# Mamba block of a four-layer graph network: rows of B and C by broadcast DMA instead of one-hot matmuls, dt products in four row groups of TensorE, and a scan that writes over its input

## The chip, the cores and the metric

The kernel runs on one core of a Trainium2 chip. The metric is the device time of the whole program in microseconds (us). The kernel before takes 3858.1 us, the median of three runs (3853.97 to 3861.62). The profile and the trace are of one execution whose span was 3854.7 us. PE is TensorE, PEld its weight loads, DVE is VectorE, ACT ScalarE, POOL GpSimd, and SP the engine whose queue issues the DMAs.

## The reference, cut to what matters

Four layers run one after the other on a graph of 3327 nodes with 256 features: a residual mean aggregation, a Mamba block behind a graph convolution, an attention layer, and two rounds of top-p attention. The change touches only the second. Its core, for a sequence of 3327 steps `t`, 512 channels `d` and 16 states `s`:

```python
h = layernorm(relu(adj @ x @ gcn_w + gcn_b))
xz = h @ w_in                       # 512 channels xc and 512 of a gate z
u = silu(causal_conv4(xc))
dbc = u @ w_xp                      # 16 columns for dt, 16 of B, 16 of C
dt = softplus(dbc[:, :16] @ w_dt + b_dt)
B, C = dbc[:, 16:32], dbc[:, 32:]
dA = exp(dt[:, :, None] * A[None])
dBu = dt[:, :, None] * B[:, None, :] * u[:, :, None]
# hst = dA_t * hst + dBu_t;  y_t = sum over s of hst[:, s] * C_t[s]
y = (ys + u * D_skip) * silu(z)
out = y @ w_out
```

All inputs are float32; in this block only the rows of B and C (see below) are kept in a shorter type.

## The kernel before

Channels lie on the 128 partitions, in four groups `g` of 128; time lies along the free axis. The 3328 (padded) steps are cut into eight chunks `c` of 128, 256, 384 and five times 512 steps (`ends`, lines 239 to 244). In each chunk the 16 states follow one another, so there are 128 pairs (chunk, state). For each pair:

- `row` (439 to 449) makes row `s` of B visible on all partitions. B and C are held as `parts`: three bfloat16 terms of each float32 number, 96 rows. One bfloat16 matmul with a one-hot stationary operand (a column of `three`) adds the three terms and copies the row to all 128 partitions in PSUM (445), and ACT copies it to SBUF (448). Rows are asked for two states ahead.
- `decay` (451 to 460) has POOL put the carried state into column 0 of each group of `db`, and ACT compute `dA = exp(A*dt)` in four activations.
- `feed` (462 to 466) is the DVE product `db = du * B` over 128 x 4w numbers, w being the chunk's width.
- `scan` (468 to 477) is one DVE recurrence over all four groups, which reads `dA` and `db` and writes `h`; POOL then copies the last column to `carry`. `dA`, `db` and `h` have two buffers each.
- `reader` (479 to 486) makes row `s` of C in PSUM by a matmul as above, and DVE multiplies `h` by it in place (549).
- Four pairs of half-matmuls against the identity add `h` to the chunk's sum in four PSUM banks `ys` (557).

Two kinds of work are woven in. `pump()` (322) advances the generator `convolve` by a step: it issues about nine of the 26 matmuls `adj @ x` of a tile of 128 nodes (264), whose operand `at` is loaded by SP (263, two buffers), then the product with `gcn_w`, the layer norm (POOL computes the power) and the transposition into `hT`. Once per state it is called, and at state 3 as often as the next chunk needs. `head(c + 1)` is advanced by one step at the end of states 3 to 14: input projection and convolution by group (four steps), then u and the 112-row product with `w_xp` (386), the split of B and C into the three terms (389 to 398 and 407: ACT casts, DVE subtractions), the dt product with `w_dt` (402, K = 16, one matmul for each group), and softplus on ACT and DVE. `gate` and `back` finish the chunk before.

PSUM has eight banks: four for `ys`, two for `ps` (rows of B, projections, `w_xp`, `w_dt`, transpositions, output product), one for `cb` of `convolve`, one for C. The framework orders instructions on each engine by the program and a priority; `tc.high_priority()` moves one ahead, `tc.keep_in_program_order` pins one. Each engine, and SP's DMA queue, runs its instructions in that order, and an instruction that waits holds those behind it. The order of the main loop is:

```python
if k < len(states): rows.append(row(*states[k]))     # k = two states ahead
if nxt: decay(*nxt)
h = scan(x, s)
...
if nxt: feed(*nxt, rows.pop(0))
nc.vector.tensor_mul(h, h, C.to_broadcast([P, NG, w]))
if nxt: C = reader(*nxt)
... # ys += h, back, gate_input, pump, head
```

Of the kernel before, what the change touches and what calls it, by code (L numbers as in the profile page):

```python
# [9 lines left out]
F32 = mybir.dt.float32  # L10
# [33 lines left out]
def gnn_kernel(ctx: ExitStack, tc: tile.TileContext, n: int, a: dict, out: bass.AP):  # L44
# [109 lines left out]
    with tc.tile_pool(name="l1b", bufs=1) as wpool, tc.tile_pool(name="l1at", bufs=2) as l1at:  # L154
# [33 lines left out]
        with tc.tile_pool(name="l1aw", bufs=1) as cwork, tc.tile_pool(name="l1c", bufs=2) as ch, \  # L188
                tc.tile_pool(name="l1t", bufs=3) as tmp, tc.tile_pool(name="l1s", bufs=2) as work, \
                tc.tile_pool(name="l1y", bufs=1, space=PSUM) as ypsum, \  # L190
                tc.tile_pool(name="l1p", bufs=2, space=PSUM) as psum, \
                tc.tile_pool(name="l1q", bufs=1, space=PSUM) as cpsum:
            def scratch():
                return tmp.tile([P, NG, 3 + WC], F32, name="t")

            gw = load(wpool, "gcn_w")
            w_dt = wpool.tile([6 * DS + DTR, DI], F32, name="w_dt")
            gb, one = w_dt[0:1, :D], w_dt[0:1, D:D + P]
# [16 lines left out]
            last = wpool.tile([P, NG, 3], F32, name="last")  # L215
            nc.vector.memset(last, 0.0)

            BC = 2 * DS
            w_sp = wpool.tile([P, NG, 3 * BC + DTR], F32, name="w_sp")
            nc.sync.dma_start(w_dt[3 * BC:, :], a["w_dt"])  # L220
            three = wpool.tile([3 * BC, BC], BF16, name="three")
            for k in range(3):
                nc.sync.dma_start(w_sp[:, :, k * BC:(k + 1) * BC], a["w_xp"][:, :, DTR:])
                nc.vector.tensor_copy(three[k * BC:(k + 1) * BC, :], ident[k * BC:(k + 1) * BC, k * BC:(k + 1) * BC])
            nc.sync.dma_start(w_sp[:, :, 3 * BC:], a["w_xp"][:, :, :DTR])

            wg = wpool.tile([P, 2, D + 2], F32, name="wg")
            nc.sync.dma_start(wg[:, :, :D], a["gat_w"])
# [16 lines left out]
            hTs, us, szs, splits = {}, {}, {}, {}  # L245

            def power(rs, var):

# [110 lines left out]
            def head(c):  # L359

                w = ends[c] - starts[c]
                xc = scratch()
                nc.gpsimd.tensor_copy(xc[:, :, :3], last)
                u = us[c] = ch.tile([P, NG, WC], F32, name="u", bufs=1)[:, :, :w]
                for g in range(NG + 1):
                    if g < NG:  # L370
                        nc.scalar.copy(xc[:, g, 3:3 + w], project(c, g, w))
# [12 lines left out]
                ps = psum.tile([P, WC], F32, name="ps")  # L384
                for g in range(NG):
                    nc.tensor.matmul(ps[:3 * BC + DTR, :w], w_sp[:, g, :], u[:, g, :],
                                     start=(g == 0), stop=(g == NG - 1))
# [12 lines left out]
                for g in range(NG):  # L400
                    ps = psum.tile([P, WC], F32, name="ps")
                    nc.tensor.matmul(ps[:, :w], w_dt[3 * BC:, g * P:(g + 1) * P], left[3 * BC:],
                                     start=True, stop=True)
                    nc.scalar.activation(v[:, g, :], ps[:, :w], AF.Identity, bias=b_dt[:, g:g + 1])
# [26 lines left out]

            dAs, dbs = ([cwork.tile([P, NG * (1 + WC)], F32, name=f"{x}{i}") for i in range(2)] for x in ("dA", "db"))

            def by_group(t, w):
                return t[:, :NG * (1 + w)].rearrange("p (g w) -> p g w", g=NG)

            def row(c, s):

                parts = splits[c]
                w = parts.shape[1]
                pb = psum.tile([P, WC], F32, name="ps")[:, :w]
                with tc.high_priority():
                    nc.tensor.matmul(pb, three[:, s:s + 1].to_broadcast([3 * BC, P]), parts, start=True, stop=True)
                B = work.tile([P, 1, WC], F32, name="row", bufs=2)[:, :, :w]
                with tc.high_priority():
                    nc.scalar.copy(B[:, 0, :], pb)  # L448
                return B

            def decay(x, s):

                c, dt, du = x
                w = dt.shape[2]
                dA, db = (by_group(x[s % 2], w) for x in (dAs, dbs))
                if s < 2 and (c == 0 or w != ends[c - 1] - starts[c - 1]):
                    nc.gpsimd.memset(dA[:, :, 0:1], 0.0)
                nc.gpsimd.tensor_copy(db[:, :, 0], carry[:, s, :])
                for g in range(NG):
                    nc.scalar.activation(dA[:, g, 1:], dt[:, g, :], AF.Exp, scale=A[:, g, s:s + 1])  # L460

            def feed(x, s, B):

                du = x[2]
                w = du.shape[2]
                nc.vector.tensor_mul(by_group(dbs[s % 2], w)[:, :, 1:], du, B.to_broadcast([P, NG, w]))  # L466

            def scan(x, s):

                w = x[2].shape[2]  # L470
                h = work.tile([P, NG * (1 + WC)], F32, name="h")
                m = NG * (1 + w)
                nc.vector.tensor_tensor_scan(h[:, :m], dAs[s % 2][:, :m], dbs[s % 2][:, :m],  # L473
                                             initial=0.0, op0=ALU.mult, op1=ALU.add)
                h = by_group(h, w)
                nc.gpsimd.tensor_copy(carry[:, s, :], h[:, :, w])
                return h[:, :, 1:]

            def reader(x, s):

                parts = splits[x[0]]
                w = parts.shape[1]
                C = cpsum.tile([P, 1, WC], F32, name="C")[:, :, :w]
                nc.tensor.matmul(C[:, 0, :], three[:, DS + s:DS + s + 1].to_broadcast([3 * BC, P]), parts,  # L484
                                 start=True, stop=True)
                return C

            def gate(c, ys):
                sz = szs[c]
# [39 lines left out]
            feed(x, 0, rows.pop(0))  # L529
            C = reader(x, 0)  # L530
            ys = ahead = None
            for c in range(nch):
                w = us[c].shape[2]
                for s in range(DS):
# [14 lines left out]
                    nc.vector.tensor_mul(h, h, C.to_broadcast([P, NG, w]))  # L549
# [781 lines left out]
```

## Time and profile before

| part of the span | from, to (us) | what |
|---|---|---|
| layer 0 | 0 to 366 | aggregation; bound by 26 x 26 matmuls of line 116 |
| layer 1 | 366 to 1641 | the stage of the change; scans (line 473) from 406.2 to 1611 |
| layers 2 and 3 | 1641 to 3855 | attention and top-p; untouched by the change |

| over the whole span | busy us | share |
|---|---|---|
| PE | 3499.9 | 91% |
| DVE | 2610.2 | 68% |
| ACT | 1738.5 | 45% |
| POOL | 494.7 | 13% |

A window's row gives, for each engine, busy time and number of instructions in that stretch, then the granted TensorE clock as a share of full speed, and DMA's share and rate. A row of the waits gives the waiting instruction, what it waited for, the total, the number of waits and the longest. A row of the timeline gives start, duration, engine, line, operation, and in brackets how long the engine had been idle and for whom. A float32 matmul stands in the trace as two records.

### The profile page before, as it was taken

The numbers are of one execution on the slowest core, as the hardware profiler recorded it, in microseconds if no ns is written. First come the engines' busy times: TensorE is split into PE (matmuls) and PEld (weight loads), VectorE is DVE, ScalarE is ACT, GpSimd is POOL, SyncE is SP. The second block draws the span as 40 slices with busy tenths as digits, with TensorE's granted clock in tenths as the row PEclk, the third lists the DMA queues.
The fourth block names the chain that finished last, engine by engine and source line by source line (L and its number), as shares of the span: only waits on it lengthen the run. The fifth ranks groups of instructions, "written<-read, shape, count | busy, mean of one in ns | idle before, by whom it ended". The sixth has DMA issues, their size and how long they took to land. (4 is left out here: it accounts for less than half of the span.)

```text
span 3854.7 us, 41751 instructions
## 1 busy us (share of the span) xinstructions
PE 3499.9 (91%) x15079; PEld 2593.0 (67%) x15079; DVE 2610.2 (68%) x5588; ACT 1738.5 (45%) x2612; POOL 494.7 (13%) x734
## 2 busy tenths in 40 slices
PE   8999999898889778689989999999999999999975
PEld 7888876554554434378868787777777667667664
DVE  1111579898988999877753445444454888888987
ACT  0000665554545465211122333333346777777773
POOL 0000122222221221111110000000001111111110
PEclk9999999998999888889999999999999999999997
DMA  7443211111111000044423222122203112221100
GB/s 231 139 134 95 84 59 53 37 46 36 42 36 36 6 0 0 15 158 139 148 73 88 62 61 56 51 59 62 59 11 101 58 56 63 64 63 54 58 23 7
DMA packets 100529, 252.96 MB, mean 66 GB/s; under 512 B 14786, under 2 KB 49090, under 8 KB 100178
## 3 DMA queue, kind: packets, MB, share of 16 engines
q1 hardware_dynamic: 100306, 250.13, 21.2%
q8 instruction: 122, 2.00, 0.2%
q14 instruction: 101, 0.83, 0.1%
HBM read 239.86 MB, written 10.22 MB: 65 GB/s over the span
## 5 line engine op out<-in xcount | busy, mean ns | idle before, releaser
L473 DVE TENSOR_TENSOR_SCAN h<-dA,db 128x2052 f32<-128x2052 f32 (+3 forms) x128 | 464.0, 3625 | 5.9 <-PE y L557 3.4
L460 ACT ACTIVATE dA<-dt,A_log 128x512 f32<-128x512 f32 (+3 forms) x512 | 297.0, 637 | 326.7 <-DVE h L473 272.7
L557 PE MATMUL y<-h,ident 128*128 128x512 f32 (+3 forms) x1024 | 436.1, 563 | 3.2 <-DVE h L549 3.2
L841 PE MATMUL acc<-G,wt 128*128 128x256 f32 x1352 | 332.7, 396 | 63.4 <-ACT wt L839 62.2
L557 PEld LDWEIGHTS y<-h,ident 128*128 128x128 f32 x1024 | 199.4, 207 | 258.0 <-issue 232.4
L839 ACT COPY wt<-tp 128x512 f32<-128x512 f32 (+1 forms) x364 | 185.9, 554 | 382.7 <-PE tp L837 382.4
L841 PE MATMUL acc<-X,wt 128*128 128x256 f32 x1352 | 343.8, 391 | 10.3 <-ACT wt L839 9.8
L841 PEld LDWEIGHTS acc<-G,wt 128*128 128x128 f32 x1352 | 254.1, 194 | 133.7 <-ACT wt L839 81.6
L809 PE MATMUL acc<-F,at 128*128 128x256 f32 x1352 | 323.1, 389 | 0.6 <-ACT q L604 0.6
L116 PE MATMUL acc<-xa,at 128*128 128x257 f32 x1352 | 310.1, 383 | 5.4 <-DMA at<-in_adjT 5.4
L841 PEld LDWEIGHTS acc<-X,wt 128*128 128x128 f32 x1352 | 242.3, 189 | 105.5 <-issue 41.3
L732 PE MATMUL acc<-F,at 128*128 128x257 f32 x1352 | 307.9, 384 | 4.9 <-DVE at L729 4.9
L264 PE MATMUL cb<-F,at 128*128 128x256 f32 x1352 | 310.6, 382 | 1.6 <-ACT hn L283 1.6
L809 PE MATMUL acc<-X,at 128*128 128x256 f32 x1352 | 309.4, 383 | 2.9 <-issue 2.9
L809 PEld LDWEIGHTS acc<-F,at 128*128 128x128 f32 x1352 | 253.8, 193 | 74.0 <-issue 40.0
L264 PEld LDWEIGHTS cb<-F,at 128*128 128x128 f32 x1352 | 257.3, 191 | 58.7 <-issue 17.7
L466 DVE TENSOR_TENSOR db<-du,row 128x2048 f32<-128x2048 f32 (+3 forms) x128 | 240.2, 1879 | 82.6 <-ACT row L448 82.5
L853 DVE MAX8 cand<-e 128x8 f32<-128x128 f32 x676 | 142.2, 281 | 226.4 <-ACT e L795 214.9
L116 PEld LDWEIGHTS acc<-xa,at 128*128 128x128 f32 x1352 | 256.7, 192 | 42.6 <-issue 5.4
L809 PEld LDWEIGHTS acc<-X,at 128*128 128x128 f32 x1352 | 255.0, 192 | 44.0 <-issue 10.9
L732 PEld LDWEIGHTS acc<-F,at 128*128 128x128 f32 x1352 | 256.4, 193 | 41.8 <-issue 5.1
L549 DVE TENSOR_TENSOR h<-h,C 128x2048 f32<-128x2048 f32 (+3 forms) x128 | 240.9, 1882 | 37.2 <-PE C L484 23.7
(305 smaller groups left out, 5303.6 us busy)
## 6 DMA issues: line engine op xcount, KB each, us to landing
at<-in_adjT SPq DMA_DIRECT2D x102, 832.0 KB, 4.5
at<-in_adjT SPq DMA_DIRECT2D x156, 448.0 KB, 3.4
at<-in_adjT SPq DMA_DIRECT2D x52, 576.0 KB, 3.8
at<-in_adjT SPq DMA_DIRECT2D x52, 320.0 KB, 3.0
at<-in_adjT SPq DMA_DIRECT2D x26, 512.0 KB, 3.5
xt<-in_xT SPq DMA_DIRECT2D x26, 128.0 KB, 4.1
qd<-q SPq DMA_DIRECT2D x104, 32.0 KB, 1.9
q<-qd SPq DMA_DIRECT2D x52, 64.0 KB, 2.3
```

The lines of the kernel that those rows point to most:

```text
L116: nc.tensor.matmul(acc, at[:, j, :], rhs[:, j0 + j, :], start=(j0 + j == 0), stop=(j0 + j == nt - 1))
L264: nc.tensor.matmul(acc, at[:, j % JC, :], X0[:, j, :], start=(j == 0), stop=(j == nt - 1))
L460: nc.scalar.activation(dA[:, g, 1:], dt[:, g, :], AF.Exp, scale=A[:, g, s:s + 1])
L466: nc.vector.tensor_mul(by_group(dbs[s % 2], w)[:, :, 1:], du, B.to_broadcast([P, NG, w]))
L473: nc.vector.tensor_tensor_scan(h[:, :m], dAs[s % 2][:, :m], dbs[s % 2][:, :m], initial=0.0, op0=ALU.mult, op1=ALU.add)
L549: nc.vector.tensor_mul(h, h, C.to_broadcast([P, NG, w]))
L557: nc.tensor.matmul(ys[g][:, :w], ident, h[:, g, :], start=False, stop=(s == DS - 1))
L732: nc.tensor.matmul(acc, at[:, j, :], F[:, j0 + j, :], start=(j0 + j == 0), stop=(j0 + j == nt - 1))
L809: nc.tensor.matmul(acc, at[:, j, :], rhs[:, j0 + j, :], start=(j0 + j == 0), stop=(j0 + j == nt - 1))
L839: nc.scalar.copy(wt[:, :m, :], pt[:, :m, :])
L841: nc.tensor.matmul(acc, wt[:, j, :], rhs[:, j0 + j, :], start=(j0 + j == 0), stop=(j0 + j == nt - 1))
L853: nc.vector.max(cand[:, s * 8:(s + 1) * 8], z[:, s * SEG:(s + 1) * SEG])
```

## The change

Its purpose is to make the rows of B and C without TensorE and ScalarE, and in full float32. Four parts belong together.

1. `w_sp` gets a new layout of its 112 output rows: the 16 dt columns stand four times, at rows 0, 32, 64 and 96, and B and C stand at rows 16 and 48. One ACT copy brings the product to SBUF (`left`); the split into three terms is gone. Two DMAs write the rows of B and C to a DRAM tile `bc` of 2 x 16 x w numbers. `row` becomes one DMA that reads row `s` of both B and C and writes it to all 128 partitions (128 x 2 x w numbers, three buffers). `reader` is gone; DVE multiplies `h` by the second half of the row.
2. `w_dt` is laid out so that group g's 16 rows start at partition 32g. The four K = 16 products use different rows of the array and are issued as two pairs, with high priority, in two steps of `head` instead of one.
3. `scan` writes over `db`; `db` has three buffers, `h` none of its own. `feed` is pinned in program order.
4. The bank of C goes to `ps`, which now has three.

```diff
-                tc.tile_pool(name="l1p", bufs=2, space=PSUM) as psum, \
+                tc.tile_pool(name="l1p", bufs=3, space=PSUM) as psum, \
+                tc.tile_pool(name="l1d", bufs=1, space=DRAM) as l1d, \
...
+            w_sp = wpool.tile([P, NG, 32 * (NG - 1) + DTR], F32, name="w_sp")
+            nc.vector.memset(w_sp, 0.0)
+            for g in range(NG):
+                nc.sync.dma_start(w_dt[32 * g:32 * g + DTR, :P], a["w_dt"][:, g * P:(g + 1) * P])
+                nc.sync.dma_start(w_sp[:, :, 32 * g:32 * g + DTR], a["w_xp"][:, :, :DTR])
+            for k in range(2):
+                nc.sync.dma_start(w_sp[:, :, 32 * k + DTR:32 * k + DTR + DS],
+                                  a["w_xp"][:, :, DTR + k * DS:DTR + (k + 1) * DS])
...
-                parts = splits[c] = ch.tile([3 * BC, WC], BF16, name="parts")[:, :w]
-                nc.scalar.copy(parts, ps[:3 * BC, :w])
-                left = scratch()[:3 * BC + DTR, 0, :w]
-                nc.scalar.copy(left, ps[:3 * BC + DTR, :w])
+                left = scratch()[:w_sp.shape[2], 0, :w]
+                nc.scalar.copy(left, ps[:w_sp.shape[2], :w])
+                bc = rows_of[c] = l1d.tile([2, DS, w], F32, name=f"bc{c}")
+                for k in range(2):
+                    nc.sync.dma_start(bc[k], left[32 * k + DTR:32 * k + DTR + DS])
                 yield None
-                nc.vector.tensor_sub(left[:3 * BC], left[:3 * BC], parts)
-                yield None
-                for k in (1, 2):
-                    nc.scalar.copy(parts[k * BC:(k + 1) * BC], left[k * BC:(k + 1) * BC])
                 v, e = (scratch()[:, :, :w] for _ in range(2))
-                for g in range(NG):
-                    ps = psum.tile([P, WC], F32, name="ps")
-                    nc.tensor.matmul(ps[:, :w], w_dt[3 * BC:, g * P:(g + 1) * P], left[3 * BC:],
-                                     start=True, stop=True)
-                    nc.scalar.activation(v[:, g, :], ps[:, :w], AF.Identity, bias=b_dt[:, g:g + 1])
-                    nc.scalar.activation(e[:, g, :], ps[:, :w], AF.Abs, bias=b_dt[:, g:g + 1])
-                yield None
-                nc.vector.tensor_sub(parts[2 * BC:], left[2 * BC:3 * BC], parts[2 * BC:])
+                for g0 in range(0, NG, 2):
+                    pair = [psum.tile([P, WC], F32, name="ps") for _ in range(2)]
+                    with tc.high_priority():
+                        for g, ps in enumerate(pair, g0):
+                            k = slice(32 * g, 32 * g + DTR)
+                            nc.tensor.matmul(ps[:, :w], w_dt[k, :P], left[k], start=True, stop=True)
+                    for g, ps in enumerate(pair, g0):
+                        nc.scalar.activation(v[:, g, :], ps[:, :w], AF.Identity, bias=b_dt[:, g:g + 1])
+                        nc.scalar.activation(e[:, g, :], ps[:, :w], AF.Abs, bias=b_dt[:, g:g + 1])
+                    yield None
...
             def row(c, s):
-                parts = splits[c]
-                w = parts.shape[1]
-                pb = psum.tile([P, WC], F32, name="ps")[:, :w]
-                with tc.high_priority():
-                    nc.tensor.matmul(pb, three[:, s:s + 1].to_broadcast([3 * BC, P]), parts, start=True, stop=True)
-                B = work.tile([P, 1, WC], F32, name="row", bufs=2)[:, :, :w]
-                with tc.high_priority():
-                    nc.scalar.copy(B[:, 0, :], pb)
-                return B
+                w = us[c].shape[2]
+                r = work.tile([P, 2, WC], F32, name="row", bufs=3)[:, :, :w]
+                nc.sync.dma_start(r, rows_of[c][None, :, s, :].to_broadcast([P, 2, w]))
+                return r
...
-                nc.vector.tensor_mul(by_group(dbs[s % 2], w)[:, :, 1:], du, B.to_broadcast([P, NG, w]))
+                tc.keep_in_program_order(nc.vector.tensor_mul(
+                    by_group(dbs[(x[0] * DS + s) % 3], w)[:, :, 1:], du, B[:, 0:1, :].to_broadcast([P, NG, w])))
...
-                h = work.tile([P, NG * (1 + WC)], F32, name="h")
+                h = dbs[(x[0] * DS + s) % 3]
-                nc.vector.tensor_tensor_scan(h[:, :m], dAs[s % 2][:, :m], dbs[s % 2][:, :m],
+                nc.vector.tensor_tensor_scan(h[:, :m], dAs[s % 2][:, :m], h[:, :m],
...
-            def reader(x, s):
...
-                        feed(*nxt, rows.pop(0))
-                    nc.vector.tensor_mul(h, h, C.to_broadcast([P, NG, w]))
-                    if nxt:
-                        C = reader(*nxt)
+                        feed(*nxt, rows[1])
+                    nc.vector.tensor_mul(h, h, rows.pop(0)[:, 1:2, :].to_broadcast([P, NG, w]))
```

More of the change, by code (lines that the diff above doesn't have):

```diff
@@ L196, in gnn_kernel @@
             gw = load(wpool, "gcn_w")
-            w_dt = wpool.tile([6 * DS + DTR, DI], F32, name="w_dt")
-            gb, one = w_dt[0:1, :D], w_dt[0:1, D:D + P]
+            w_dt = wpool.tile([32 * (NG - 1) + DTR, P + D + P], F32, name="w_dt")
+            gb, one = w_dt[0:1, P:P + D], w_dt[0:1, P + D:]
             nc.sync.dma_start(gb, bass.AP(tensor=a["gcn_b"].tensor, offset=a["gcn_b"].offset, ap=[[0, 1], [1, D]]))
@@ L216, in gnn_kernel @@
             nc.vector.memset(last, 0.0)
[L218 to L225, printed above, removed]
+            w_sp = wpool.tile([P, NG, 32 * (NG - 1) + DTR], F32, name="w_sp")
[6 more added lines that the diff above has]
+                                  a["w_xp"][:, :, DTR + k * DS:DTR + (k + 1) * DS])
             wg = wpool.tile([P, 2, D + 2], F32, name="wg")
@@ L244, in gnn_kernel @@
             starts = [0] + ends[:-1]
-            hTs, us, szs, splits = {}, {}, {}, {}
+            hTs, us, szs, rows_of = {}, {}, {}, {}
             def power(rs, var):
@@ L385, in head @@
                 for g in range(NG):
-                    nc.tensor.matmul(ps[:3 * BC + DTR, :w], w_sp[:, g, :], u[:, g, :],
+                    nc.tensor.matmul(ps[:w_sp.shape[2], :w], w_sp[:, g, :], u[:, g, :],
                                      start=(g == 0), stop=(g == NG - 1))
-                parts = splits[c] = ch.tile([3 * BC, WC], BF16, name="parts")[:, :w]
-                nc.scalar.copy(parts, ps[:3 * BC, :w])
-                left = scratch()[:3 * BC + DTR, 0, :w]
-                nc.scalar.copy(left, ps[:3 * BC + DTR, :w])
+                left = scratch()[:w_sp.shape[2], 0, :w]
@@ L429, in gate_input @@
                 nc.scalar.copy(szs[c][:, g, :], project(c, NG + g, w))
-            dAs, dbs = ([cwork.tile([P, NG * (1 + WC)], F32, name=f"{x}{i}") for i in range(2)] for x in ("dA", "db"))
+            dAs, dbs = ([cwork.tile([P, NG * (1 + WC)], F32, name=f"{x}{i}") for i in range(m)]
+                        for x, m in (("dA", 2), ("db", 3)))
             def by_group(t, w):
@@ L454, in decay @@
                 w = dt.shape[2]
-                dA, db = (by_group(x[s % 2], w) for x in (dAs, dbs))
+                dA, db = by_group(dAs[s % 2], w), by_group(dbs[(c * DS + s) % 3], w)
                 if s < 2 and (c == 0 or w != ends[c - 1] - starts[c - 1]):
@@ L477, in scan @@
                 return h[:, :, 1:]
-            def reader(x, s):
[L481 to L486, printed above, removed]
             def gate(c, ys):
@@ L528, in gnn_kernel @@
             decay(x, 0)
-            feed(x, 0, rows.pop(0))
-            C = reader(x, 0)
+            feed(x, 0, rows[0])
             ys = ahead = None
```

## The prediction

> **What bounds the kernel now.** I read the busy time of each engine chunk by chunk first, then DVE's waits, then the timeline around the longest. Windows cut near the first scans of chunks 0, 2, 4 and 6:
>
> ```profile
> core 0: us, PE busy (x) PEld busy (x) DVE busy (x) ACT busy (x) POOL busy (x), PEclk, DMA share, GB/s
> 406.00:487.00 81.00, 77.61 (x445) 65.76 (x444) 52.79 (x74) 54.16 (x143) 14.40 (x45) 1.00 0.28 85
> 599.00:749.00 150.00, 139.37 (x494) 90.74 (x493) 131.53 (x87) 86.72 (x153) 37.64 (x52) 0.93 0.15 46
> 930.00:1112.00 182.00, 160.22 (x499) 91.31 (x498) 165.83 (x91) 93.03 (x147) 43.41 (x50) 0.93 0.13 38
> 1294.00:1450.00 156.00, 116.99 (x294) 56.24 (x295) 145.71 (x76) 91.53 (x161) 38.94 (x38) 0.86 0.00 0
> ```
>
> In chunk 0 PE is full (77.6 of 81) and DVE waits; from chunk 2 on DVE is the fuller engine (166 of 182 in chunk 4), PE close behind (160), ACT half idle. So a saving is what DVE's waits are worth, as long as PE's own work fits. DVE's waits over the eight chunks (406 to 1618):
>
> ```profile
> DVE db L466 <- ACT row L448: 82.5, 23, 12.9
> DVE h L549 <- PE C L484: 23.7, 9, 6.9
> DVE h L549 <- POOL carry L476: 9.6, 22, 1.3
> DVE h L473 <- PE y L557: 3.4, 4, 2.3
> ```
>
> Over 80% of DVE's 132 us of idle time (1212 less 1080 busy) is waiting for a row of B or C. By chunk, rows of B and C cost: 24.8, 15.5, 14.9, 14.6, 14.6, 14.6, 7.2, 0 us. The 14.6 is nearly one event that recurs in chunks 3, 4 and 5 with the same length (and 10.8 us in chunk 2). Its timeline in chunk 3:
>
> ```profile
> 870.63 4.43 DVE L473 TENSOR_TENSOR_SCAN h<-dA,db 128x2052 f32<-128x2052 f32 x1
> ...
> 877.45 2.07 PE L402 MATMUL ps<-t,w_dt 16*128 16x512 f32 x2 [6.12 <-ACT hT L306]
> ...
> 880.71 0.72 ACT L460 ACTIVATE dA<-dt,A_log 128x512 f32<-128x512 f32 x1
> ...
> 887.57 0.69 ACT L404 ACTIVATE t<-ps,b_dt 128x512 f32<-128x512 f32 x1 [2.74 <-PE ps L402]
> ...
> 889.33 0.63 PE L445 MATMUL ps<-parts,three 96*128 96x512 bf16 x1
> ...
> 890.00 0.59 ACT L448 COPY row<-ps 128x512 f32<-128x512 f32 x1 [1.16 <-PE ps L445]
> ...
> 890.62 4.58 DVE L466 TENSOR_TENSOR db<-du,row 128x2048 f32<-128x2048 f32 x2 [12.92 <-ACT row L448]
> ```
>
> With two `ps` banks, the dt products wait for ACT to empty one, ACT waits for the products, PE runs slowly after its pause, and the row's matmul and copy stand behind all of it. `dA`, the scan's other input, was ready at 881.4.
>
> **What the skill says.** *TensorE: Matmul & The Clock Gate*, Part 1: after an idle window of about 3.4 us the array runs at half clock until it has been busy as long. The trace agrees: after 6.12 us idle two half-products of 512 columns take 2.07 us, while the records at 960 us show eight in 3.60. *VectorE: DVE Perf Modes*, the perf-mode tier table: a float32 product of two tensors runs at one element a cycle from SBUF and PSUM alike, so C in SBUF should not make line 549 faster; lines 466 (SBUF) and 549 (PSUM) below agree, 2277 and 2282 ns. *DMA: Bandwidth & Descriptors*, Rules for kernel authors: a leading broadcast dimension of c copies confines a DMA to c engines; here it is 128, so all 16 serve it. No run shows that yet. *TensorE: Matmul & The Clock Gate*, Part 3: products with K up to 32 in distinct row groups run concurrently; nothing in this trace does so.
>
> **The change part by part.** The groups concerned (406 to 1620; busy us, mean ns):
>
> ```profile
> L466 DVE TENSOR_TENSOR db<-du,row 128x2048 f32<-128x2048 f32 x80 | 182.2, 2277 | 48.6 <-ACT row L448 48.5
> L549 DVE TENSOR_TENSOR h<-h,C 128x2048 f32<-128x2048 f32 x80 | 182.6, 2282 | 9.1 <-POOL carry L476 4.1 <-PE C L484 2.5
> L445 PE MATMUL ps<-parts,three 96*128 96x512 bf16 x80 | 34.2, 434 | 34.5 <-ACT row L448 13.5 <-ACT t L371 10.2 <-ACT sz L429 5.7
> L448 ACT COPY row<-ps 128x512 f32<-128x512 f32 x80 | 46.4, 580 | 25.6 <-PE ps L445 25.5
> ```
>
> *Removed from DVE:* the two subtractions of the split, 0.68 us each, 1.36 in each of the five heads of 512 and 8.3 over all (directly on DVE's line), and the waits above. *Removed from ACT:* 128 row copies, 46.4 + 7.5 + 5.8 + 3.4 = 63 us, and some 10 us of casts; worth nothing by itself, as ACT is half idle. *Removed from PE:* 256 one-hot matmuls. The records give them 47.4 + 45.8 = 93 us, but at 951.91 one starts and at 952.13 the next matmul starts, so a slot is 0.22 us when PE is full: 160 x 0.22 plus some 0.15 for each of the narrower 96 is about 50 us. The dt products are 41 us busy; two at a time saves at most half, 20 us, or nothing if they don't overlap. All of it counts only where PE is the bound, chunks 0 and 1.
>
> *Added: DMA.* 128 row loads, 512 KB each at w = 512, 54 MB in all, and 16 stores of 32 KB or less. The nearest rows:
>
> ```profile
> at<-in_adjT SPq DMA_DIRECT2D x26, 512.0 KB, 3.5
> qd<-q SPq DMA_DIRECT2D x104, 32.0 KB, 1.9
> t<-in_attn_dst SPq DMA_DIRECT2D x1, 128.0 KB, 5.6
> ```
>
> 512 KB lands in 3.5 us. A source row read 128 times could be slower: the broadcast load `attn_dst` took 5.6 us, but beside other loads, and in the trace's packet records its 1 KB packets take 46 ns, the median of all 1 KB packets. 2 KB packets take 87 ns, so 256 of them over 16 engines are 1.4 us of transfer. I take 3.5 us and keep 6 as the upper end. Against that stands the lead: row s+2 can be issued when the product of state s-1 frees its buffer, and is needed after scan s+1, i.e. after two scans and two products, 4.4 + 4.6 + 4.4 = 13.4 us. At w = 128 the lead is some 4 us, about the latency, but PE bounds that chunk. The load is 54 MB in some 1130 us, 48 GB/s beside the present 31 to 85. So the loads are hidden. The DRAM store and first load (1.9 + 3.5 us) run beside softplus, which takes 13 us in `head(0)` and six states later on.
>
> *Added wait: SP's queue.* Behind a waiting `at` load (line 263) queue the row loads, for which `feed` waits. The `at` loads wait up to 32 us for PE now, but with nothing behind them. In program order an `at` load waits for matmuls issued two or three pumps earlier, which PE has done about when the row's own buffer comes free; so I count nothing, and keep it as the rival that ends slower.
>
> *Moved: buffers.* `feed` s+1 now waits for the sums of state s-2, a scan later than `scan` s did before (3.4 us of waits), so that is easier. POOL's copy into column 0 waits for the same sums, and `carry` stands behind it; the 9.6 us of waits for `carry` stay. Scanning in place changes no count of elements: 4425 ns stay. The third `ps` bank removes the knot of 870 to 890 together with the row; the pair's products in two steps leave ACT free for `dA`. I leave 1.5 us a chunk for `dA` arriving late, as 881.4 against 880.0 in the event above, where `feed` would then end.
>
> *The sum.* Chunks 3, 4, 5: 14.6 + 1.36 - 1.5 = 14.5 each, 43 us. Chunk 2: 14.9 less some 2 for PE (139 of 150), 13. Chunk 6: 4.7 + 2.5 + 1.4 less 1, 7.5. Chunk 7 has no such wait and no head: 0. Chunks 0 and 1 are PE's: chunk 0 saves its removed matmuls, 32 x 0.15, 5 us; chunk 1 (PE 102, DVE 90 of 112) loses 9 us of recorded matmuls and part of its gaps, 11 us. `head(0)`: the split's steps in front of the dt product, 2 us. Together 81.5 us: 3858.1 - 81.5 = 3776.6, about 3777.
>
> **The rivals.** *All waits go.* DVE runs through in chunks 0 and 1 too: 82.5 + 23.7 + 8.3 = 114.5, 3744. Against it: PE's 77.6 of 81. *The knot stays in another form:* ACT, still in order, waits on the dt products with `dA` behind, so that chunks 2 to 5 win only the subtractions and the short waits. 81.5 less 12.9 x 3 + 10.8 = 49.5 leaves 32: 3826. For it: PE, emptier, will be at half clock more often. *PE is the true bound throughout* (160 of 182): the saving is its removed 50 us, 3808; against it, 117 of 156 in chunk 6. *SP's queue makes rows late:* if every second of the 76 `at` loads held up a row so that `feed` waits 3.5 us, 133 us are added against 82 won: 3909. For it: `at` loads wait 901 us in all on SP; against it, the lead of 13.4 us.
>
> **How the numbers follow.** As forecast, within 20 us: 0.58. All waits gone: 0.11. Knot or PE bound: 0.20. Rows late: 0.08, and something that cancels the gain: 0.03. The range reaches from the all-gone rival's 3744 to the knot's 3826 and leaves out the slower ones and a little below. Faster by over 0.2% (7.7 us): 0.88; within: 0.04; slower: 0.08.
>
> **What would show it.** Right: no row of DVE waiting for a row's DMA above some us in chunks 2 to 7; a distance of some 168 us between the first scans of chunks 3, 4, 5 (now 182); row loads of 512 KB landing in 3.5 to 6 us; scan and products at 4425 and 2280 ns. Wrong: `feed` waiting for DMA; `scan` waiting for `dA` by 5 us or more at each head; rows landing later than 13 us; L557's sums holding `feed`.

## The result and the profile after

| | median (us) | range of the four runs | ratio to before, 95% interval |
|---|---|---|---|
| before | 3856.4 | 3854.0 to 3861.6 | |
| after | 3827.0 | 3821.1 to 3831.8 | 0.9921 [0.9903, 0.9939] |

The change wins 29 us where 81.5 were forecast, and the time lies 1 us outside the range. The profiled execution after has a span of 3829.9 us, 24.8 less than the 3854.7 of before. I split both spans at the first scan of each chunk. The columns 0 to 7 are the time from a chunk's first scan to the next chunk's (for chunk 7, to the end of the last scan), in us:

| | first scan at | 0 | 1 | 2 | 3 | 4 | 5 | 6 | 7 | after the last scan |
|---|---|---|---|---|---|---|---|---|---|---|
| before | 406.2 | 81.3 | 111.5 | 149.8 | 181.4 | 182.0 | 182.0 | 174.4 | 143.0 | 2243.3 |
| after | 394.5 | 74.5 | 115.8 | 148.1 | 181.2 | 181.1 | 181.0 | 165.4 | 145.3 | 2243.1 |
| won | 11.7 | 6.8 | -4.3 | 1.7 | 0.2 | 0.9 | 1.0 | 9.0 | -2.3 | 0.2 |
| forecast | 2 | 5 | 11 | 13 | 14.5 | 14.5 | 14.5 | 7.5 | 0 | 0 |

So the layers behind are as they were, and the gain comes from what lies before the first scan, from chunk 0 and from chunk 6. The three chunks in which the forecast saw half of its gain won 2 us together. Chunks 0, 1, 4 and 6 after, as windows (the columns are those of the windows before):

```profile
394.52:469.01 74.49, 73.30 (x404) 62.29 (x403) 51.53 (x71) 50.18 (x123) 17.70 (x45) 1.00 0.41 115
469.01:584.79 115.78, 103.52 (x429) 82.14 (x430) 91.74 (x79) 62.41 (x125) 28.87 (x53) 0.93 0.39 100
914.04:1095.13 181.09, 153.22 (x466) 88.91 (x465) 165.69 (x89) 83.06 (x129) 46.97 (x50) 0.92 0.29 86
1276.11:1441.52 165.41, 123.62 (x306) 59.90 (x305) 162.90 (x84) 90.04 (x163) 55.01 (x40) 0.86 0.20 52
```

In chunk 6, DVE is now full (162.9 of 165.4). In chunk 4 PE has lost 7 us of work and ACT 10, and the length is the same to 0.9 us: DVE still stands idle for 15 us of 181. DVE's waits after, from 365 to 1620 us, show for what:

```profile
DVE db L462 <- PE y L542: 50.4, 14, 9.2
DVE db L536 <- POOL carry L473: 30.5, 57, 1.9
DVE u L377 <- ACT u L372: 17.2, 11, 4.8
...
DVE db L462 <- DMA row<-bc: 0.5, 1, 0.5
```

The 106 us of waits for rows of B and C are gone, and the DMA that brings them now is waited for once, 0.5 us. In their place `feed` (L462) waits 50.4 us for the sums (L542), and the product by C (L536) 30.5 us for POOL's `carry`. The groups of the stage, shapes kept apart (mean ns after the busy time):

```profile
L470 DVE TENSOR_TENSOR_SCAN db<-dA,db 128x2052 f32<-128x2052 f32 x80 | 353.8, 4423 | 1.2
L536 DVE TENSOR_TENSOR db<-db,row 128x2048 f32<-128x2048 f32 x80 | 183.0, 2288 | 19.6 <-POOL carry L473 17.6
L462 DVE TENSOR_TENSOR db<-du,row 128x2048 f32<-128x2048 f32 x80 | 182.1, 2276 | 27.9 <-PE y L542 27.3
L403 PE MATMUL ps<-t,w_dt 16*128 16x512 f32 x40 | 15.4, 858 | 23.6 <-ACT t L389 23.6
```

DVE's three operations cost what they did. The DMAs, from the page (KB each, median us to landing):

```profile
row<-bc SPq DMA_DIRECT2D x80, 512.0 KB, 4.9
...
row<-bc SPq DMA_DIRECT2D x16, 256.0 KB, 4.9
```

And the event that fills the room of the row's: `feed` waits for the sums 9.1 us in chunk 4, 9.2 in chunk 3 and 9.0 in chunk 5. This is the timeline of chunk 4 after:

```profile
1025.12 2.29 DVE L462 TENSOR_TENSOR db<-du,row 128x2048 f32<-128x2048 f32 x1
1025.26 2.20 POOL L473 COPY carry<-db 128x4 f32<-128x4 f32 x1 [9.47 <-DVE mv L85]
...
1027.49 2.29 DVE L536 TENSOR_TENSOR db<-db,row 128x2048 f32<-128x2048 f32 x1
1027.66 2.20 POOL L251 TENSOR_SCALAR rs<-mv 128x1 f32<-128x1 f32 x1
...
1029.70 4.43 DVE L470 TENSOR_TENSOR_SCAN db<-dA,db 128x2052 f32<-128x2052 f32 x1
...
1029.94 4.54 POOL L252 TENSOR_TENSOR rs<-rs,mhalf 128x1 f32<-128x1 f32 x1
1032.24 1.02 PE L542 MATMUL y<-db,ident 128*128 128x512 f32 x2
1034.59 0.26 POOL L294 TENSOR_SCALAR nb<-mv,rs 128x1 f32<-128x1 f32 x1
...
1034.89 0.60 ACT L297 ACTIVATE hn<-hn,nb,rs 128x256 f32<-128x256 f32 x1 [11.33 <-POOL nb L294]
...
1036.79 2.56 ACT L456 ACTIVATE dA<-dt,A_log 128x512 f32<-128x512 f32 x4
1039.25 0.56 ACT L389 COPY t<-ps 112x512 f32<-112x512 f32 x1
...
1039.86 2.08 PE L403 MATMUL ps<-t,w_dt 16*128 16x512 f32 x4 [6.60 <-ACT t L389]
...
1041.87 4.46 PE L542 MATMUL y<-db,ident 128*128 128x512 f32 x6
...
1046.37 2.29 DVE L462 TENSOR_TENSOR db<-du,row 128x2048 f32<-128x2048 f32 x1 [9.07 <-PE y L542]
```

Read it from the end. `feed` at 1046.37 needs a `db` buffer, and all three hold states whose sums are not done. Those sums (six of eight records) stand on PE behind the dt products (L403), which `high_priority` put in front of them. The dt products wait 6.60 us for `left` (L389); afterwards PE is slow, as in the event of before: six records of the sums take 4.46 us, where eight take 3.60 a little later. `left` stands on ACT behind `dA` and a pinned normalization of `convolve` (L297), which holds ACT for 11.33 us because POOL is late with its power: 128 numbers take 2.20 us beside the product by C and 4.54 beside the scan. While DVE stands idle, at 953.12 in the same trace, the same two steps take 0.22 and 0.57 us.

### The profile page after: what moved, and what is told of

The parts are those of the page before. It is cut to its first block, busy times and chain, and to the rows that moved or that the text cites. A ratio compares the mean times of both kernels' runs of the same rounds, so it can differ in the third digit from the quotient of the medians.

```text
span 3829.9 us, 41271 instructions
## 1 busy us (share of the span) xinstructions
PE 3452.1 (90%) x14823; PEld 2574.3 (67%) x14823; DVE 2607.4 (68%) x5570; ACT 1666.6 (44%) x2460; POOL 538.6 (14%) x734
## 5 line engine op out<-in xcount | busy, mean ns | idle before, releaser
L542 PE MATMUL y<-db,ident 128*128 128x512 f32 (+3 forms) x1024 | 445.1, 580 | 59.2 <-DVE db L536 59.2
L470 DVE TENSOR_TENSOR_SCAN db<-dA,db 128x2052 f32<-128x2052 f32 (+3 forms) x128 | 463.9, 3624 | 5.0 <-ACT dA L456 1.6
L542 PEld LDWEIGHTS y<-db,ident 128*128 128x128 f32 x1024 | 205.1, 215 | 261.1 <-issue 166.5
L266 PEld LDWEIGHTS cb<-F,at 128*128 128x128 f32 x1352 | 257.0, 191 | 56.7 <-issue 17.6
L462 DVE TENSOR_TENSOR db<-du,row 128x2048 f32<-128x2048 f32 (+3 forms) x128 | 240.5, 1879 | 54.8 <-PE y L542 50.4
L536 DVE TENSOR_TENSOR db<-db,row 128x2048 f32<-128x2048 f32 (+3 forms) x128 | 241.7, 1888 | 34.8 <-POOL carry L473 30.5
```

Source lines behind the costliest of these rows:

```text
L266: nc.tensor.matmul(acc, at[:, j % JC, :], X0[:, j, :], start=(j == 0), stop=(j == nt - 1))
L462: tc.keep_in_program_order(nc.vector.tensor_mul(by_group(dbs[(x[0] * DS + s) % 3], w)[:, :, 1:], du, B[:, 0:1, :].to_broadcast([P, NG, w])))
L470: nc.vector.tensor_tensor_scan(h[:, :m], dAs[s % 2][:, :m], h[:, :m], initial=0.0, op0=ALU.mult, op1=ALU.add)
L536: nc.vector.tensor_mul(h, h, rows.pop(0)[:, 1:2, :].to_broadcast([P, NG, w]))
L542: nc.tensor.matmul(ys[g][:, :w], ident, h[:, g, :], start=False, stop=(s == DS - 1))
```

## The experiments

All are compared with the kernel before, run beside them. Chunk lengths in us, counted as above, waits of DVE in us from 365 to 1620. Line numbers shift by a few from edit to edit, so that L535 or L543 can be the product that is L536 after the change.

| kernel | median (us) | ratio [95%] | chunks 1, 2 | 3, 4, 5 | `feed` for sums | product for `carry` |
|---|---|---|---|---|---|---|
| after | 3827.0 | 0.9921 [0.9903, 0.9939] | 115.8, 148.1 | 181.2, 181.1, 181.0 | 50.4 | 30.5 |
| rows of B and C apart | 3827.4 | 0.9928 [0.9912, 0.9945] | 113.0, 145.2 | 181.3, 180.7, 180.9 | 51.6 | 30.4 |
| the same, four `db` | 3816.4 | 0.9911 [0.9890, 0.9932] | 119.6, 146.7 | 180.9, 172.9, 172.8 | 32.4 | 28.5 |
| dt without priority | 3799.5 | 0.9855 [0.9837, 0.9873] | 111.1, 142.3 | 171.4, 171.0, 171.5 | 20.4 | 31.0 |
| normalization later | 3799.9 | 0.9858 [0.9842, 0.9875] | 112.8, 147.5 | 168.6, 174.1, 175.9 | 29.3 | 28.7 |
| both of these | 3809.6 | 0.9887 [0.9871, 0.9904] | 112.5, 146.2 | 171.7, 175.0, 176.1 | 31.0 | 26.2 |
| both, `carry` on DVE | 3799.9 | 0.9860 [0.9844, 0.9877] | 114.5, 147.2 | 168.2, 170.1, 170.3 | 37.9 | none |
| no priority, `carry` on DVE | 3801.8 | 0.9860 [0.9842, 0.9878] | 107.2, 141.2 | 173.6, 174.2, 174.1 | 27.9 | none |
| two `ps` banks | 3830.1 | 0.9940 [0.9919, 0.9961] | 114.9, 149.0 | 180.3, 181.3, 181.2 | 57.7 | 29.7 |
| C in PSUM | 3826.8 | 0.9927 [0.9902, 0.9951] | 115.1, 153.8 | 175.5, 179.0, 181.2 | 35.2 | 22.0 |
| C in PSUM, no priority | 3798.4 | 0.9847 [0.9820, 0.9874] | 112.7, 147.5 | 169.6, 172.3, 172.4 | 29.5 | 19.5 |
| loads twice | 3851.5 | 0.9989 [0.9982, 0.9996] | 116.4, 148.2 | 181.2, 181.1, 181.0 | 53.6 | 30.3 |
| before, normalization later | 3876.9 | 1.0064 [1.0047, 1.0081] | 114.5, 155.7 | 186.2, 185.9, 185.1 | none | 9.8 |

The time behind the last scan, which no edit touches, lies between 2235.7 and 2246.2 us in these profiles. So a few us between two medians say little unless the chunks carry them.

My theory after the result was the chain just read: POOL late, so ACT late, so the dt products late, so the sums behind them late, so no buffer for `feed`. Rivals: DVE has no slack left and other work fills any gap; the added loads or SP's queue cost the time; the buffers or banks are too few. Each link can be cut by itself.

**Is it the buffers?** A fourth `db` fits only if the rows take less room, so B and C are loaded apart (two buffers of B, one of C); the control does only that.

```diff
-                        for x, m in (("dA", 2), ("db", 3)))
+                        for x, m in (("dA", 2), ("db", 4)))
...
-                r = work.tile([P, 2, WC], F32, name="row", bufs=3)[:, :, :w]
+                r = work.tile([P, 1, WC], F32, name="row", bufs=2)[:, :, :w]
...
+            Crow = cwork.tile([P, 1, WC], F32, name="Crow")
+            def reader(x, s):
...
+                nc.sync.dma_start(Crow[:, :, o:o + w], rows_of[c][None, 1:2, s, :].to_broadcast([P, 1, w]))
```

> The changed kernel with four buffers of db instead of three. To make room the rows are loaded as two DMAs, B two states ahead in two buffers and C one state ahead in one buffer. Theory 1 (in the head's step with the dt product, POOL's slow layer-norm chain holds ACT, ACT holds the copy of the 112-row product, the dt matmuls stand on TensorE ahead of the sums of y, and feed waits for those sums because it needs their buffer): with a fourth buffer feed has nine us more, the wait of feed for the sums falls from 50 us to under 10, and chunks 3, 4 and 5 take some 172 us each instead of 181; the whole 3795 to 3805, if late rows of C in chunks 0 to 2 do not give some of it back. Theory 2 (TensorE's own work fills the chunk, the wait only shows it): the wait moves to another instruction, chunks 3 to 5 stay at 180 to 182 us.

> Control for the run with four buffers: the same split loads of the rows of B and C, but three buffers of db as in the changed kernel. Both theories: chunks 3, 4 and 5 at 181 us as in the changed kernel, with feed waiting about 9 us for the sums in each; chunks 0 and 1 may be up to 2 us a state longer where a row of C comes late. 3825 to 3850.

The control is `after` again: 3827.4. With four buffers `feed`'s wait for the sums is gone from chunk 4 (9.4 in the control, 0), and chunks 4 and 5 are 8 us shorter. Chunk 3 is not, and chunk 1 is 7 us longer than the control. So in chunks 4 and 5 the missing buffer is what turns the late sums into idle time, but 3816.4 is 11 us less than the control, at overlapping intervals of the ratios, and it leaves the sums late.

**Is it the dt products' place on PE?** The kernel after with one line taken away:

```diff
-                    with tc.high_priority():
-                        for g, ps in enumerate(pair, g0):
-                            k = slice(32 * g, 32 * g + DTR)
-                            nc.tensor.matmul(ps[:, :w], w_dt[k, :P], left[k], start=True, stop=True)
+                    for g, ps in enumerate(pair, g0):
+                        k = slice(32 * g, 32 * g + DTR)
+                        nc.tensor.matmul(ps[:, :w], w_dt[k, :P], left[k], start=True, stop=True)
```

> The changed kernel without the high priority of the dt matmuls, so that they stand in program order behind the sums of y. Theory 1: the sums no longer stand behind a matmul that waits for ACT; the wait of feed for the sums falls from 50 us to under 10, chunks 3 to 5 take 172 us each, 3795 to 3805. Theory 2: no change beyond 5 us, 3822 to 3832.

3799.5, 28 us less than after, the intervals far apart. All of DVE's waits in chunk 4 of this kernel:

```profile
DVE db L535 <- POOL carry L472: 4.7, 9, 1.9
```

and its window:

```profile
902.00:1073.00 171.00, 149.66 (x466) 87.70 (x464) 165.47 (x89) 83.24 (x129) 47.11 (x50) 0.94 0.32 90
```

DVE is busy for 165.5 of 171.0 us. Yet the normalization still holds ACT for 75.6 us over the stage, where it was 90.5 with the priority, and at worst for 11.8 in place of 11.3:

```profile
ACT hn L297 <- POOL nb L294: 75.6, 16, 11.8
```

So in this order a held ACT costs DVE little; it costs DVE's time through the products that PE puts in front of the sums. In front of the first scan the priority helps: without it this scan starts at 398.6 us in place of 394.5.

**Is it the normalization on ACT?** It is moved one `pump` further, next to the transposition, so that POOL has a state more:

```diff
-                    rest = [measure, norm, turn]
+                    def late(norm=norm, turn=turn):
+                        norm()
+                        turn()
+                    rest = [measure, lambda: None, late]
```

> The changed kernel with the normalization of a tile in the convolution (the ACT instruction that waits for POOL's power) moved one step later, next to the transposition that uses it. Theory 1: ACT's waits for POOL there fall from 90 us to under 25, the copy of the 112-row product is not held, and feed's wait for the sums goes: 3790 to 3805. Theory 2: ACT's waits fall but the time stays at 3822 to 3832.

3799.9: the same gain, from the other end of the chain. ACT's waits of `hn` for `nb` fall from 90.5 to 2.1 us, and chunks 3 to 5 are 5 to 13 us shorter.

**Do the two add up?**

> The changed kernel without the priority of the dt matmuls and with the late normalization. Each of the two alone gave about 3800. Theory 1 (both release the same knot): together little more than one, 3790 to 3800, chunks 3 to 5 at 168 to 172 us. Rival (they remove two different waits): the savings of 27 us add up, 3773.

They don't: 3809.6, worse than either alone, and neither number of the expectation. One knot has two ends; cutting it twice wins nothing. The second cut gives the order another shape, in which DVE's statistics wait 32.6 us for `relu` on ACT (L285), up to 11.5 at a time; it was 13.4 without priority and 8.7 with the later normalization. That the 10 us lost come from that wait is not shown; no run isolates it.

**Is `carry` the rest?** DVE makes the copy itself:

```diff
-                nc.gpsimd.tensor_copy(carry[:, s, :], h[:, :, w])
+                nc.vector.tensor_copy(carry[:, s, :], h[:, :, w])
```

with both edits above, and with the missing priority alone:

> As the run with both, and the last column of each scan is copied to carry by DVE instead of POOL. Theory 1: what is left of DVE's waits is mostly the wait of the product with C for that copy on POOL (some 30 us); DVE pays 128 copies of some 0.1 to 0.15 us, 13 to 19 us: 3775 to 3790. Rival (the wait for POOL hides another that ends at the same time): same as the run with both or up to 15 us slower.

> The changed kernel without the priority of the dt matmuls and with the last column of each scan copied to carry by DVE instead of POOL (without the late normalization, which took away from the run with both). In the run with late normalization 16 such copies took 2.6 us of DVE in a chunk; the waits for POOL were 4.7. Theory 1 (these waits are DVE's last large one in chunks 3 to 5): 168.5 to 170 us a chunk instead of 171, the whole 3785 to 3798. Rival (ACT or TensorE is next at the same time): 3795 to 3805, no change.

The copy costs DVE some 165 ns, and the waits for `carry` vanish in both. On top of both edits it wins 10 us (3809.6 to 3799.9); on top of the missing priority nothing (3801.8 against 3799.5; in the profiles the last scan ends at 1562.9 us against 1552.9): 27.9 us of `feed` waiting for sums and 17.6 us of the scan waiting for `dA` stand in their place. The 30 us of waits for `carry` are no 30 us to be had.

**Are the loads hidden?** Each row is loaded twice into the same buffer; the second load starts after the first has landed.

```diff
-                nc.sync.dma_start(r, rows_of[c][None, :, s, :].to_broadcast([P, 2, w]))
+                for _ in range(2):
+                    nc.sync.dma_start(r, rows_of[c][None, :, s, :].to_broadcast([P, 2, w]))
```

> The changed kernel with each load of a row issued twice, the second into the same buffer after the first has landed, so that the row is there some 5 us later and twice as many bytes move. Theory 1 (the loads are hidden, with 13.4 us of lead at 512 columns): chunks 3 to 7 as in the changed kernel within 1 us; in chunks 0 and 1, where the lead is 4 to 8 us, up to 3 us a state more: 3827 to 3870 in all, all of the difference in chunks 0 to 2. Rival (rows or the bytes are near the bound already): chunks 3 to 5 grow by over 5 us each and feed waits for DMA.

3851.5, but chunks 2 to 7 are equal to those of after to 0.1 us. The cost is in chunk 0 (95.4 against 74.5 us) and in front of it (4.3 us). DVE's wait for the rows over the stage:

```profile
DVE db L463 <- DMA row<-bc: 30.1, 12, 4.5
```

Of these waits, 22.5 us lie in chunk 0, 3.1 in front of it and 4.5 in chunk 1, which is 0.6 us longer (116.4 against 115.8). So from chunk 2 on the lead is enough for a load of twice the length, and no cost of SP's order shows. In chunk 0 a row has the length of two states, 9.3 us (74.5 / 16 is 4.7 for one): one load fits, two after each other don't.

**Is it the third bank?**

```diff
-                tc.tile_pool(name="l1p", bufs=3, space=PSUM) as psum, \
+                tc.tile_pool(name="l1p", bufs=2, space=PSUM) as psum, \
```

> The changed kernel with two banks of ps instead of three (the eighth bank stays unused). Theory 1 (the third bank is what made the first head 7 to 12 us shorter and helps TensorE past ACT): the first scan starts at 400 to 406 us instead of 394.5, and chunks 2 to 5 are longer by 2 to 6 us each, as each pair of dt products then waits for both banks: 3840 to 3855. Rival (the bank is of no use once no row goes through it): 3822 to 3832.

3830.1, its interval overlapping that of after, and the chunks the same to 2.2 us: no gain of the third bank can be told.

**Was the knot of before the same one?** The later normalization alone, in the kernel before:

> The kernel before with the late normalization alone. Theory 1 (the stall of 12.9 us in chunks 3 to 5 of the kernel before comes from two PSUM banks and ACT waiting for the dt products with the row behind, another knot than that of the changed kernel): the stall stays, 3845 to 3860. Rival (it is the same hold of ACT by POOL's chain in both kernels): the stall goes, some 40 us less, 3815.

3876.9, slower than before (ratio 1.0064 [1.0047, 1.0081]). The row's waits grow from 82.5 to

```profile
DVE db L469 <- ACT row L451: 107.5, 30, 15.0
```

So POOL's late normalization was not the start of the event of 870 to 890. In its trace the dt products are held up for free banks and by a transposition. What fell with the rows of B was replaced by an event with a start of its own.

**Does the product by C hold up POOL?** In the trace of before, the same normalization in chunk 4 looks like this:

```profile
1031.51 2.26 DVE L549 TENSOR_TENSOR h<-h,C 128x2048 f32<-128x2048 f32 x1
1031.68 0.22 POOL L249 TENSOR_SCALAR rs<-mv 128x1 f32<-128x1 f32 x1 [2.52 <-DVE mv L85]
1031.99 0.57 POOL L250 TENSOR_TENSOR rs<-rs,mhalf 128x1 f32<-128x1 f32 x1
1032.66 0.27 POOL L292 TENSOR_SCALAR nb<-mv,rs 128x1 f32<-128x1 f32 x1
```

Beside the product by C, POOL ran at full speed there: C lay in PSUM. After the change both operands lie in SBUF. Over the stage, POOL's first step took 0.22 us when it began beside that product before (14 times; once, at its very end, the scan behind it made it 3.42) and 1.88 on average after (15 times). To test what it is worth, C goes back to PSUM, now by ACT from the loaded row, in the bank that two `ps` set free:

```diff
-                tc.tile_pool(name="l1p", bufs=3, space=PSUM) as psum, \
+                tc.tile_pool(name="l1p", bufs=2, space=PSUM) as psum, \
...
+            def reader(r, w):
+                C = cpsum.tile([P, 1, WC], F32, name="C")[:, :, :w]
+                nc.scalar.copy(C[:, 0, :], r[:, 1, :])
+                return C
...
-                    nc.vector.tensor_mul(h, h, rows.pop(0)[:, 1:2, :].to_broadcast([P, NG, w]))
+                    nc.vector.tensor_mul(h, h, C.to_broadcast([P, NG, w]))
+                    if nxt:
+                        C = reader(rows.pop(0), nxt[0][2].shape[2])
```

> The changed kernel with two ps banks (worth nothing by themselves, 3830) and, in the bank set free, C's row in PSUM: ACT copies the second half of the loaded row there (128 copies, some 63 us of ACT), and the product by C reads db from SBUF and C from PSUM as it did before the change. Theory 1: the product by C became a product of two SBUF operands through the change, and POOL's normalization, which now takes 1.88 us beside it where it took 0.22, is delayed by it into the scan; that is what holds the normalization on ACT for 11.3 us in place of 6.1. Then POOL's first step beside the product by C is back at 0.2 us, ACT's waits for the normalization fall from 90 to some 50 us, DVE's waits for carry from 30 to some 10, and the time is 3800 to 3815. Theory 2: the normalization is as late as before the scan anyway, and what holds the dt products is only their place in the order: chunks 3 to 5 stay at 180 to 182 us, and the time is 3825 to 3840, the upper end through the copies on ACT.

> The same, and the dt products without high priority (3799.5 alone). Theory 1: DVE's waits for carry (31 us there) fall to some 10 as well, and the time is 3780 to 3792. Theory 2: the copies on ACT only put something more in front of dA, and the time is 3798 to 3815.

For POOL and ACT it is as theory 1 has it. The timeline with C in PSUM, chunk 4:

```profile
1033.12 2.28 DVE L543 TENSOR_TENSOR db<-db,C 128x2048 f32<-128x2048 f32 x1
1033.33 0.22 POOL L251 TENSOR_SCALAR rs<-mv 128x1 f32<-128x1 f32 x1
1033.64 0.57 POOL L252 TENSOR_TENSOR rs<-rs,mhalf 128x1 f32<-128x1 f32 x1
1034.31 0.26 POOL L294 TENSOR_SCALAR nb<-mv,rs 128x1 f32<-128x1 f32 x1
1034.61 0.60 ACT L297 ACTIVATE hn<-hn,nb,rs 128x256 f32<-128x256 f32 x1 [5.51 <-POOL nb L294]
```

ACT is held for 5.51 us in place of 11.33, over the stage 58.9 in place of 90.5 (before the change it was 49.3), and in that chunk DVE's waits begin with

```profile
DVE t L416 <- ACT t L414: 4.7, 1, 4.7
DVE db L543 <- POOL carry L479: 3.4, 7, 1.7
DVE db L468 <- PE y L551: 1.9, 2, 1.7
```

`feed` waits 1.9 us for the sums in place of 9.1. But the time is theory 2's, 3826.8: ACT is 9 us busier in this chunk (91.9 against 83.1) and a new wait of 4.7 us for the softplus on ACT takes most of what the sums gave back; chunk 2 is 5 us longer than with two banks alone. Without priority the two versions are equal (3798.4 and 3799.5). The expected fall of the waits for `carry` to 10 us didn't come either (22.0 and 19.5).

The best versions are the ones without priority, at 3799.5 and 3798.4; which of the two is faster can't be told. Two parts of the change were not tested by themselves: the pin of `feed` in program order, and the scan over its input against one into a tile of its own. What they are worth stays open.

## Why the prediction was wrong, and where it was right

**What held.** DVE bounds the stage from chunk 2 on, and the rows' waits vanished: 106 us became 0.5. The loads are hidden: 4.9 us to landing lies between the forecast's 3.5 and 6, and even twice that is hidden from chunk 2 on. "In program order an `at` load waits for matmuls ... so I count nothing" held too. The in-place scan stayed at its length (4425 ns before, 4423 after) and the products at theirs (2282 and 2288 for C). "At most half, 20 us" for the dt products was reached and a little more: their busy time over all widths went from 41.9 us (34.3 + 3.6 + 2.3 + 1.7) to 19.6 (15.4 + 1.8 + 1.4 + 1.0). That is what *TensorE: Matmul & The Clock Gate*, Part 3, says of distinct row groups, and this trace agrees: two products start 0.01 us apart. Chunk 6, in which `convolve` has one normalization left to do, is the forecast's clean case: 7.5 us forecast, 9.0 measured.

**The step that failed** is "The third `ps` bank removes the knot of 870 to 890 together with the row; the pair's products in two steps leave ACT free for `dA`". No gain of the bank can be told (3830 with two). The row left the knot, but the dt products stayed in it, and the change put them in front of the sums by `high_priority`. I described that line and priced it nowhere: I asked who waits on ACT for the dt products, and not what stands behind them on PE. What stands there is the sums; "L557's sums holding `feed`" is in my list of signs of being wrong, but without a price. For these sums `feed` waits because of the second failing step, "a scan later than `scan` s did before (3.4 us of waits), so that is easier". With three buffers shared by `db` and `h`, the waits for sums went from 3.4 to 50.4 us. Taking the priority away, or the normalization out of ACT's way, gives 27 to 28 us back; a fourth buffer takes chunk 4's wait away. In chunks 3, 4 and 5 this is the term that was mis-sized: 14.5 us each forecast, 0.2, 0.9 and 1.0 measured, 10.0, 11.0 and 10.5 without priority.

**A cost that I set at nothing.** I asked whether C in SBUF makes the product faster, found that it doesn't, and left it there. *SBUF — State Buffer*, Who interferes with whom, says that a DVE instruction with two SBUF inputs contends with a GpSimd instruction that reads SBUF, and that such contention is an exclusive lock; one with a single SBUF input does not contend. The traces agree on both sides: 0.22 and 0.57 us beside the product with C in PSUM, 2.20 beside the product with both in SBUF and 4.54 beside the scan behind it. In chunk 4 ACT is held twice as long with it (11.33 us against 5.51). It is shown to feed the knot (C in PSUM: `feed`'s wait in chunk 4 falls to 1.9 us). What it is worth in time is not shown: the run that undoes it also puts copies on ACT, and its time stays at 3826.8.

**The half clock.** Its role was foreseen for the rival only ("PE, emptier, will be at half clock more often"). *TensorE: Matmul & The Clock Gate*, Part 1, fits again: after 6.60 us idle, two products in parallel take 2.08 us, where they take 1.13 in the same trace at 1057.16. In chunk 1 PE's mean clock went from 0.98 to 0.93; before, its window was

```profile
487.50:599.00 111.50, 101.80 (x456) 79.01 (x455) 89.35 (x78) 66.56 (x137) 29.11 (x52) 0.98 0.21 62
```

So PE was busy for 103.5 us with 429 records, where 456 had taken 101.8. "Chunk 1 ... 11 us" failed: PE had less to do and was not done sooner, and the chunk grew by 4.3 us, with 7.1 us of DVE waiting for `u` from ACT and 5.9 for sums. The clock alone does not set the length: with two banks it is 0.96 in chunk 1 and the chunk takes 114.9 us, without priority it is 0.95 and the chunk is as long as before (111.1). Which part each of these has stays open.

**`carry`.** "The 9.6 us of waits for `carry` stay" failed: 30.5. Without priority this is 4.7 us of chunk 4 where before had 0.9, a difference about as large as the 3.5 us by which that chunk misses its forecast (171.0 against 182.0 - 14.5 = 167.5). But moving the copy gave nothing alone, so I don't book it as a loss of its own.

**Too small.** The first head and what leads to it won 11.7 us where I put 2. Of this, 6.2 us are won in front of the stage: layer 0 ends at 359.3 us in place of 365.6. In the trace of before, PE waits 4.7 us there for DVE at 66.8, and DVE 5.4 us for the load of `attn_dst`, which the attention layer needs; after, DVE waits 1.8 us for that load. Layer 0 ends between 358.7 and 359.9 us in all kernels with the change, and at 363.6 in the kernel before with the later normalization. Why the load comes in time, no run shows. From the product with `w_sp` to the first scan it was 17.2 us and is 12.4 (from 388.98 to 406.22, from 382.11 to 394.52). Without priority it is 17.0 (from 381.56 to 398.55), although the split is gone there too: nearly all of these 4.8 us is the priority's, and the 2 us that I put for the split's steps don't show by themselves. The third bank is not their cause (the first scan starts at 394.7 with two). Chunk 7 lost 2.3 us that I can't place.

**The sum.** Forecast 81.5, measured 24.8 by the profile: chunks 3 to 5 miss 40.9, chunk 1 15.3, chunk 2 11.3 and chunk 7 2.3, and the start, chunk 0 and chunk 6 are 13.0 better. The rival that hit, "the knot stays in another form", gave 3826 with a chance inside the 0.20, and the upper end of the range was set at exactly its value, so that the result fell just outside. That it came so near is in part luck: it shares the forecast's 11 us for chunk 1 and 2 for the start, and the miss of 15.3 in the one is in good part balanced by the 9.7 too many in the other. Its number was nearly right, its picture in part: ACT did wait, but for POOL, and `dA` was in time; DVE waited for PE. One term was summed wrongly: the two subtractions take 8.8 us of DVE over the seven heads and not 8.3, which moves only the rival in which all waits go, by under 1 us.

## What to carry to other kernels

When a wait is taken out of a loop, look at what else waits in the same event, and follow it on every engine's queue: a producer that is moved ahead by priority while its own input is late holds everything behind it, here the sums that free a buffer. Before an operand is moved from PSUM to SBUF, ask who works beside that instruction, not only how long it takes. Where a wait has two or three causes in a row, cut one and measure; here cutting two gave less than one.

## What was not expected of the hardware

- POOL's small operations last about as long as the DVE product or scan of two SBUF operands beside which they begin: 128 x 4 numbers take 0.19 us alone and 2.20 beside a 2.29 us product, 128 x 1 take 0.57 alone and 4.54 beside a scan of 4.43. With one operand in PSUM there is no such effect (0.22 and 0.57). `feed` held POOL in both kernels: the copy to `carry` that began beside it took 1.89 us on average before (39 times) and after (33 times).
- One row of B and C written to all 128 partitions lands in 4.9 us at 512 KB and at 256 KB alike, beside the other loads of the kernel, so at these sizes its length is not set by the bytes alone.
